# Attention scores from a two-half query: four terms stacked on 128 rows, or three terms on 64 rows with two heads side by side

## The chip, the core and the metric

The kernel runs on one NeuronCore of a Trainium2 chip. Five engines work from queues of their own, in order: TensorE (PE in the profile; its weight loads are the row PEld) multiplies, ScalarE (ACT) evaluates the exponentials and copies results out of the accumulators, VectorE (DVE) does elementwise work and reductions, GpSimd (POOL) issues the transfers that gather and scatter rows by index, and SyncE (SP) issues the plain transfers. Matmul results land in an accumulator memory, PSUM, of eight banks; everything else is in SBUF, whose 128 partitions are the rows of a tile. The metric is the device time of one launch in microseconds (us); lower is better.

## The reference

Sixteen batches of 1024 tokens with 512 features, 8 heads of width 64, and a 0/1 mask per token. The query is also the key and the value.

```python
xt = jnp.transpose(x, (0, 2, 1))
q = xt @ Wq.T
qh = q.reshape(B, T, NH, dk).transpose(0, 2, 1, 3)
scores = scale * jnp.einsum('bhqd,bhkd->bhqk', qh, qh)
logits = (scores * cmask + (1.0 - cmask) * NEG) * rmask
attn = jax.nn.softmax(logits, axis=-1)
ctx = jnp.einsum('bhqk,bhkd->bhqd', attn, qh)
out = ctx @ Wo.T
return x + jnp.transpose(out, (0, 2, 1))
```

A masked key takes no part, and a masked query averages over all keys, so the kernel computes attention for the unmasked tokens alone and gives every masked token the projected mean.

## The kernel before

Per batch the unmasked tokens (384 to 544 of 1024) are gathered into a tile of A = 544, 528 or 512 columns. PE transposes the rows (L486), multiplies by the query weights in float16 halves (L513: high times high, low times high, high times low), and ACT writes the float32 query `q`, 128 rows by A columns for each pair of heads e = 0..3 (head 2e in rows 0 to 63, head 2e+1 in rows 64 to 127).

`qsplit` (L521) cuts `q` into float16 halves: DVE casts the high half (L529), subtracts for the low half (L530) and copies the high half once more (L531), with a short extra copy (L534) where A is 528. Four DMAs on SP's queue (L540 to L543) then build `xx`, which holds for each head two stacks of 128 rows: high over low, and low over high. With these stacks as operands one matmul of 128 rows adds two of the four products of halves, so the scores of one head need two matmuls (a = 0, 1) for each half of the columns (g = 0, 1): four matmuls of A/2 columns (L701). Their result, `pss`, is one tile of two PSUM banks; the pool `ps_s` has two such tiles, used in turn. ACT takes the exponential out of it (L705), with the running sum read afterwards as an instruction of its own (ACTIVATION_READ_ACCUMULATOR), and the next scores that use that tile wait for it.

Each batch has 16 steps: a pair of heads p = 0..3 and a row block i = 0..3. In a step the scores of head 2p come first, then a part of the filling work (`fill`: queries, values and transposes of the next batch, projections of the previous one), then the scores of head 2p+1, then another part. The 16 matmuls of probabilities times values (`attend`, L726; two passes each in float32, so 32 records) run together at the second step of the next pair. They write 64 columns of the array each, two heads side by side, into the upper and lower halves of `pav`. Slots over 512 are the tail: their scores for four heads go together (L676, weights 32 columns wide, 16 matmuls, twice a batch in 14 batches). `value` (L559) makes the value tiles by multiplying both halves of `xx` by `two`, two identities of 64 columns on top of each other (L569, moving 64 columns, 8 per call). Program order within an engine is set by the tile framework when the kernel is built, from the order of the calls, priorities and its own estimates; on the chip every engine takes its queue in that order.

Of the kernel before, what the change touches and what calls it, by code (L numbers as in the profile page):

```python
# [19 lines left out]
P = 128  # L20
# [3 lines left out]
DK = 64  # L24
# [3 lines left out]
SCALE = 0.125  # L28
NEG = -1.0e30

C = 544
CT = C - 512
CQ = C + 2
HG = H // 2
# [12 lines left out]
class Fast:  # L47
# [91 lines left out]
    def setup2(self):  # L139
        nc, fixed = self.nc, self.fixed  # L140

        self.quad = fixed("quad", [P, HG])
        nc.vector.tensor_reduce(self.quad, self.ident.rearrange("p (r t) -> p r t", r=HG), AX.X, ALU.add)
        self.xh = fixed("xh", [P, DC, CQ], F16)
        self.xl = fixed("xl", [P, DC, CQ], F16)
        for t in (self.xh, self.xl):
            nc.gpsimd.memset(t[:, :, C + 1:], 0.0)

        self.rcol = [fixed("rcol%d" % k, [P, P]) for k in range(2)]
        self.smcol = [fixed("smcol%d" % k, [P, P]) for k in range(2)]  # L150
        for t in self.rcol + self.smcol:
            nc.gpsimd.memset(t, 0.0)

        self.two = fixed("two", [P, DK], F16)
        nc.vector.tensor_tensor(self.two, self.ident[:, :DK], self.ident[:, DK:], ALU.add)

        self.big = fixed("big", [P, self.B + 2 * DC])

        self.par = fixed("par", [P, 2])
        nc.vector.tensor_tensor(self.par, self.quad[:, 0:2], self.quad[:, 2:4], ALU.add)  # L160

        self.low = fixed("low", [P, 1])
        nc.vector.tensor_reduce(self.low, self.ident.rearrange("p (r k t) -> p k r t", r=HG, k=2)[:, 1], AX.XY, ALU.add)
        self.sign = fixed("sign", [P, 1])
        nc.vector.tensor_scalar(self.sign, self.low, -2.0, 1.0, ALU.mult, ALU.add)
# [243 lines left out]
            s["xt"] = self.rows(s["idx"][:s["A"] - 512, 4:5], self.sb([P, D], F32, "xt"))  # L409

    def start(self, b):
        s = self.st[b] = {"xa": [], "xx": [], "v": [], "c": [], "nm": [], "corr": [], "xm": []}
        s["ms2"] = self.sb([P, 2 * DC], F32, "ms2", 2)

    def load_half(self, b, k, after=None):
# [105 lines left out]
    def qsplit(self, b, e):  # L521


        nc, s = self.nc, self.st[b]
        A = s["A"]
        q = s["q"][:, e, :A]
        full = self.sb([P, 3, C], F16, "hl", 2)
        hl = full[:, :, :A]
        nc.vector.tensor_copy(hl[:, 0, :], q)  # L529
        nc.vector.tensor_tensor(hl[:, 1, :], q, hl[:, 0, :], ALU.subtract)  # L530
        nc.vector.tensor_copy(hl[:, 2, :], hl[:, 0, :])  # L531
        S = C if A > 512 else A
        if A < S:
            nc.vector.tensor_copy(full[:, :, A:], full[:, :, 512:A])  # L534
            hl = full
        xx = self.sb([P, 4, C], F16, "xx", 5)[:, :, :S]

        def spread():
            lo, up = slice(0, DK), slice(DK, P)
# [5 lines left out]
        self.later(spread)  # L545
        s["xx"].append(xx)

    def squares(self, v, dst, act=False, first=False):
        nc = self.nc
# [9 lines left out]
    def value(self, b, e):  # L559
        nc, s = self.nc, self.st[b]  # L560
        if e == 0:
            s["sd"] = self.sb([P, DC, H], F32, "sd")
        pv = self.pm([P, 4, P])
        for k in range(4):
            if b == 0:
                nc.tensor.transpose(pv[:, k, :], s["q"][:, e, k * P:(k + 1) * P], self.ident)
            else:
                for h in range(2):
                    nc.tensor.matmul(pv[:, k, h * DK:(h + 1) * DK], lhsT=s["xx"][e][:, 2 * h, k * P:(k + 1) * P],  # L569
                                     rhs=self.two, start=True, stop=True)  # L570
# [90 lines left out]
    def scores(self, b, p, i):  # L661


        nc, s = self.nc, self.st[b]
        A = s["A"]
        CH = A // 2
        if "z" not in s:
            s["z"] = self.sb([P, H, 4], F32, "z", 2)
            s["zt"] = self.sb([P, 2], F32, "zt", 2)
        if i is None:  # L670
            pt = self.ps_s.tile([P, 2, 512], F32, tag="s", name="pss")
            for a in range(2):
                for g in range(2):
                    for r in range(HG):
                        xx, k = s["xx"][2 * p + r // 2], r % 2
                        self.beat = nc.tensor.matmul(pt[r * CT:(r + 1) * CT, g, :CH], lhsT=xx[:, 2 * k, 512:C],  # L676
                                                     rhs=xx[:, 2 * k + a, g * CH:(g + 1) * CH],
                                                     start=(a == 0), stop=(a == 1)).ins
            t = self.sb([P, C], F32, "p", 12)[:, :A]
            nc.scalar.activation(t.rearrange("p (g c) -> p g c", g=2), pt[:, :, :CH], AF.Exp,  # L680
                                 bias=s["nm"][p][:, HG:], scale=SCALE, accum_out=s["zt"][:, p:p + 1])

            hi = self.sb([P, C], F32R, "c", 4)[:, :A]
            lo = t.bitcast(F32R)
            nc.vector.tensor_copy(hi, t)
            nc.vector.tensor_tensor(lo, t, hi.bitcast(F32), ALU.subtract)

            def spread():
                s["pt"] = self.sb([P, 2, C], F32R, "pt")[:, :, :A]
                half = slice(0, DK), slice(DK, P)  # L690
# [8 lines left out]
        for a in range(2):  # L699
            for g in range(2):  # L700
                self.beat = nc.tensor.matmul(pt[:, g, :CH], lhsT=xx[:, 2 * k, i * P:(i + 1) * P],  # L701
                                             rhs=xx[:, 2 * k + a, g * CH:(g + 1) * CH],
                                             start=(a == 0), stop=(a == 1)).ins
        t = self.sb([P, C], F32, "p", 12)[:, :A]
        self.exp = [nc.scalar.activation(t.rearrange("p (g c) -> p g c", g=2), pt[:, :, :CH], AF.Exp,  # L705
                                         bias=s["nm"][p // HG][:, p % HG:p % HG + 1], scale=SCALE,
                                         accum_out=s["z"][:, p, i:i + 1]).ins]
        return t

    def attend(self, b, p, i, ps):  # L710
        nc, s = self.nc, self.st[b]
# [221 lines left out]
    def run(self, flag):  # L933
        B = self.B
        L = lambda f, *a: lambda: f(*a)
        S = [(p, i) for p in range(NP) for i in range(4)]
# [21 lines left out]
        for i, e in enumerate(ends):  # L958
            g = list(range(ends[i - 1] + 1 if i else 0, e + 1))
# [36 lines left out]
        g1 = [(0, L(self.gather, 1, j)) for j in range(5)]  # L996

        def rest1():
            with self.behind(self.last_xx):
                for k in range(DC, 2 * DC):  # L1000
                    self.load_half(1, k)

# [32 lines left out]
        if True:  # L1035
            for b in range(B + 1):
                o, n = b - 1, b + 1
# [17 lines left out]
                if n < B:  # L1055
# [22 lines left out]
                    if b == 0:  # L1078
                        k = next(k for k, (c, f) in enumerate(m) if f is index[0][1])
# [40 lines left out]
                for st, (p, i) in enumerate(S):  # L1120
# [3 lines left out]
                    if i is None:  # L1124
                        if self.wide[b] > 512:
                            self.scores(b, p, None)
                    else:
                        ps = [self.scores(b, 2 * p, i)]
                        if i == 2 and whole:
                            whole.pop()()  # L1130
                    fill(share[st][0], st == N - 1)
                    if i is not None:
                        ps.append(self.scores(b, 2 * p + 1, i))

                    for _ in range(1 if b < B - 2 else -(-len(self.urgent + self.spare) // (N - st))):
                        self.issue()

# [165 lines left out]
```

## Time and profile before

| | |
|---|---|
| median of 2 runs | 1030.3 us (1029.69 and 1030.91) |
| span of the profiled execution | 1032.2 us |
| PE busy | 988.2 us (96%), 8455 matmuls |
| VectorE busy | 725.1 us (70%) |
| ScalarE busy | 659.5 us (64%) |
| GpSimd busy | 300.8 us (29%) |
| bytes moved by DMA | 177.73 MB |

The profile is one execution recorded on the chip. A group's row gives the line, the engine, the operation and its tiles, the count, the busy time, the mean duration of one, and the engine's idle time before it with what ended that idle time. A matmul's recorded duration includes the way through the array, which overlaps with the next matmul: what a matmul costs in a dense stretch is the distance from its start to the next start, and the timeline, which merges a run of equal instructions into one row (start, length from the first start to the last end, count), is the view to take it from. Idle time of an engine that is not the bottleneck costs nothing.

### The profile page before, as it was taken

Reading aid. Unit: us, or ns where it says so; the run is one execution under the profiler, and the core shown is the slowest. Engines: PE = TensorE matmul, PEld = TensorE weight load, DVE = VectorE, ACT = ScalarE, POOL = GpSimd, SP = SyncE. Lnnn points to the kernel's source line nnn. Section 1 sums busy time; section 2 is a strip of 40 time slices with the busy share of each in tenths; the row PEclk is TensorE's granted clock in tenths of the full one; section 3 lists DMA queues with packets and bytes.
Section 4 is the critical chain, followed back from the end, with each engine's and each line's share of the span. In section 5 each row is a group of like instructions: output and inputs, shape, how many; then the busy total and the mean of one; then the engine's idle time right before and its main releaser. Section 6 shows DMA issues by size and latency. Waiting matters only on the chain. (4 is left out here: it accounts for less than half of the span.)

```text
span 1032.2 us, 23511 instructions
## 1 busy us (share of the span) xinstructions
PE 988.2 (96%) x8455; PEld 685.0 (66%) x8455; DVE 725.1 (70%) x2410; ACT 659.5 (64%) x1702; POOL 300.8 (29%) x307
## 2 busy tenths in 40 slices
PE   7798999999999999999999999999999999999996
PEld 6576667666676766767666676767666666776563
DVE  6897668676775767877666787767777777666653
ACT  5876767557667666667667567756667667665550
POOL 3101013223311232233232333323232322325562
PEclk9999999999999999999999999999999999999999
DMA  6746546557554586575657565576565666556652
GB/s 199 231 139 183 136 134 161 183 161 206 165 142 128 150 239 172 151 209 148 190 157 227 172 169 168 163 203 185 163 210 138 192 184 184 151 142 191 185 183 95
DMA packets 78795, 177.73 MB, mean 172 GB/s; under 512 B 14688, under 2 KB 20576, under 8 KB 78672
## 3 DMA queue, kind: packets, MB, share of 16 engines
q1 hardware_dynamic: 57584, 108.40, 38.8%
q0 software_dynamic: 21088, 67.75, 20.9%
q8 instruction: 69, 1.13, 0.5%
q14 instruction: 54, 0.44, 0.1%
HBM read 91.49 MB, written 33.91 MB: 121 GB/s over the span
## 5 line engine op out<-in xcount | busy, mean ns | idle before, releaser
L705 ACT ACTIVATE p<-pss,nm 128x528 f32<-128x528 f32 (+2 forms) x512 | 359.5, 706 | 169.6 <-PE pss L701 160.0
L701 PE MATMUL pss<-xx 128*128 128x264 f16 (+2 forms) x2048 | 300.9, 276 | 6.1 <-ACT p L705 5.2
L726 PE MATMUL pav<-p,v 128*64 128x264 f32 (+2 forms) x2048 | 243.3, 390 | 0.0
L701 PEld LDWEIGHTS <-xx 128*128 128x128 f16 x2048 | 194.2, 99 | 62.4 <-issue 25.1
L726 PEld LDWEIGHTS pav<-p,v 128*64 128x64 f32 x2048 | 141.4, 137 | 85.7 <-issue 13.5
L901 POOL DMA_INDIRECT y_out<-xa,idx x68 | 73.5, 1081 | 285.4 <-PE pss L701 101.6
L513 PE MATMUL pm<-xh,wqh 128*128 128x264 f16 (+5 forms) x512 | 142.2, 278 | 4.1 <-DVE xa L822 3.4
L513 PE MATMUL pm<-xl,wqh 128*128 128x264 f16 (+5 forms) x512 | 141.6, 277 | 0.2 <-DVE xl L445 0.2
L513 PE MATMUL pm<-xh,wql 128*128 128x264 f16 (+5 forms) x512 | 141.7, 277 | 0.0
L395 POOL DMA_INDIRECT xa<-x_in,idx x68 | 68.6, 1009 | 201.7 <-PE pss L701 81.1
L513 PEld LDWEIGHTS <-wqh 128*128 128x128 f16 x1024 | 98.3, 99 | 24.0 <-issue 7.5
L705 ACT ACTIVATION_READ_ACCUMULATOR p<-pss,nm 128x1 f32 x512 | 103.9, 203 | 0.0
L901 POOL DMA_INDIRECT y_out<-xi,idx x60 | 72.6, 1211 | 97.0 <-PE pss L701 26.5
L817 PE MATMUL pm<-woh,ch 128*128 128x512 f16 x240 | 91.1, 379 | 0.0
L817 PE MATMUL pm<-woh,cl 128*128 128x512 f16 x240 | 90.9, 379 | 0.0
L817 PE MATMUL pm<-wol,ch 128*128 128x512 f16 x240 | 90.9, 379 | 0.0
L395 POOL DMA_INDIRECT xi<-x_in,idx x60 | 61.3, 1021 | 95.3 <-PE pss L701 31.9
L516 ACT ACTIVATE q<-pm 128x264 f32<-128x264 f32 (+5 forms) x128 | 50.2, 392 | 59.9 <-PE pm L513 59.3
L822 DVE SCALAR_TENSOR_TENSOR xa<-pm,xa 128x512 f32<-128x512 f32 x60 | 41.3, 689 | 56.4 <-PE pm L817 52.7
L817 PEld LDWEIGHTS <-ch 128*128 128x128 f16 x480 | 46.1, 98 | 44.8 <-issue 0.9
L799 DVE TENSOR_TENSOR c<-c,rb 128x528 f32<-128x528 f32 (+2 forms) x64 | 45.4, 710 | 43.0 <-DMA rb<-rd 21.3
L888 DVE TENSOR_TENSOR xi<-xi,ub 128x512 f32<-128x512 f32 (+1 forms) x60 | 40.8, 688 | 41.8 <-PE pss L701 41.2
(223 smaller groups left out, 1509.6 us busy)
## 6 DMA issues: line engine op xcount, KB each, us to landing
xx<-hl SPq DMA_DIRECT2D x224, 136.0 KB
xm<-x_nat_in SPq DMA_DIRECT2D x56, 512.0 KB
rb<-rd SPq DMA_DIRECT2D x72, 132.0 KB
rb<-rd SPq DMA_DIRECT2D x40, 136.0 KB
pt<-c SPq DMA_DIRECT2D x36, 132.0 KB
pt<-p SPq DMA_DIRECT2D x36, 132.0 KB
ub<-ud SPq DMA_DIRECT2D x16, 256.0 KB
xx<-hl SPq DMA_DIRECT2D x32, 128.0 KB
```

The source lines that it names most:

```text
L395: dma = self.nc.gpsimd.indirect_dma_start(out=tile[:n], out_offset=None, in_=self.x, in_offset=bass.IndirectOffsetOnAxis(ap=idx, axis=0))
L513: self.beat = nc.tensor.matmul(pq, lhsT=w[:, c, e * P:(e + 1) * P], rhs=xx[:, c, cols], start=(k == 0), stop=(k == 3 * DC - 1)).ins
L516: nc.scalar.activation(s["q"][:, e, cols], pq, AF.Copy, scale=1.0 / (SX * SW))
L701: self.beat = nc.tensor.matmul(pt[:, g, :CH], lhsT=xx[:, 2 * k, i * P:(i + 1) * P], rhs=xx[:, 2 * k + a, g * CH:(g + 1) * CH], start=(a == ...
L705: self.exp = [nc.scalar.activation(t.rearrange("p (g c) -> p g c", g=2), pt[:, :, :CH], AF.Exp, bias=s["nm"][p // HG][:, p % HG:p % HG + 1 ...
L726: mm = nc.tensor.matmul(s["pav"][k * DK:(k + 1) * DK, g, :CH], lhsT=s["v"][p][:, i, k * DK:(k + 1) * DK], rhs=ps[k][:, cols], start=(i == ...
L799: self.once(nc.vector.tensor_tensor(c[:, :A], c[:, :A], s["rb"][p], ALU.mult), self.beat if p < 3 else None)
L817: nc.tensor.matmul(po[:cols.stop - cols.start], lhsT=a[:, e, cols], rhs=w[:, e, :], start=(e == 0 and k == 0), stop=(e == DC - 1 and k == 2))
L822: self.nc.vector.scalar_tensor_tensor(x, po, 1.0 / (SX * SW), x, ALU.mult, ALU.add)
L888: self.once(self.nc.vector.tensor_tensor(x[:n], x[:n], s["ub"][:n], ALU.add), self.beat)
L901: dma = self.nc.gpsimd.indirect_dma_start(out=self.out, out_offset=bass.IndirectOffsetOnAxis(ap=idx, axis=0), in_=x, in_offset=None)
```

## The change

- `qsplit` writes the two halves, high and low, into `hl` (now 6 buffers, 2 slots) and nothing else: the second copy of the high half, the extra copy, the four DMAs and `xx` are gone.
- `scores` makes both heads of a pair in one call: three products of halves (high high, high low, low high; low low is left out, in this kernel's computation, as in its query and output products), each with 64 rows. For each product and each half of the columns the matmul of head 0 (rows 0 to 63) is followed by that of head 1 (rows 64 to 127). They write two `pss` tiles, and the two exponentials follow: 12 matmuls for two heads instead of 8.
- The loop calls `scores` once per step, ahead of the first part of the filling, instead of once before and once after it.
- For the tail, `qsplit` makes `tk` on VectorE: the tail columns of the halves times a 0/1 mask for the rows of one head, one instruction where A is 544 and two where it is 528. The tail scores then take 24 matmuls of 128 rows instead of 16.
- `value` adds two products with a 128-wide identity (moving 128 columns instead of 64), again 8 per call.

```diff
         q = s["q"][:, e, :A]
-        full = self.sb([P, 3, C], F16, "hl", 2)
-        hl = full[:, :, :A]
-        nc.vector.tensor_copy(hl[:, 0, :], q)
-        nc.vector.tensor_tensor(hl[:, 1, :], q, hl[:, 0, :], ALU.subtract)
-        nc.vector.tensor_copy(hl[:, 2, :], hl[:, 0, :])
...
-        xx = self.sb([P, 4, C], F16, "xx", 5)[:, :, :S]
...
-            nc.sync.dma_start(out=xx[lo, 0:2, :], in_=hl[lo, 0:2, :])
-            nc.sync.dma_start(out=xx[up, 0:2, :], in_=hl[lo, 1:3, :])
-            nc.sync.dma_start(out=xx[lo, 2:4, :], in_=hl[up, 0:2, :])
-            self.last_xx = nc.sync.dma_start(out=xx[up, 2:4, :], in_=hl[up, 1:3, :]).ins
...
+        hl = self.sb([P, 2, C], F16, "hl", 6)
+        nc.vector.tensor_copy(hl[:, 0, :A], q)
+        nc.vector.tensor_tensor(hl[:, 1, :A], q, hl[:, 0, :A], ALU.subtract)
+        s["hl"].append(hl)
+        if A > 512:
+            if e % 2 == 0:
+                s["tk"].append(self.sb([P, 2, 2, 2, CT], F16, "tk", 3))
+            n, st = A - 512, s["tk"][e // 2][:, e % 2]
+            for r in range(CT // n):
+                self.last_hl = nc.vector.tensor_tensor(
+                    st[:, :, :, r * n:(r + 1) * n], hl[:, :, 512:A].unsqueeze(2).broadcast_to([P, 2, 2, n]),
+                    self.par16.unsqueeze(1).unsqueeze(3).broadcast_to([P, 2, 2, n]), ALU.mult).ins
...
                 for h in range(2):
-                    nc.tensor.matmul(pv[:, k, h * DK:(h + 1) * DK], lhsT=s["xx"][e][:, 2 * h, k * P:(k + 1) * P],
-                                     rhs=self.two, start=True, stop=True)
+                    nc.tensor.matmul(pv[:, k, :], lhsT=s["hl"][e][:, h, k * P:(k + 1) * P], rhs=self.id16,
+                                     start=(h == 0), stop=(h == 1))
...
-        xx, k = s["xx"][p // 2], p % 2
-        pt = self.ps_s.tile([P, 2, 512], F32, tag="s", name="pss")
-        for a in range(2):
+        hl = s["hl"][p]
+        pts = [self.ps_s.tile([P, 2, 512], F32, tag="s", name="pss") for _ in range(2)]
+        for k, (a, c) in enumerate(((0, 0), (0, 1), (1, 0))):
             for g in range(2):
-                self.beat = nc.tensor.matmul(pt[:, g, :CH], lhsT=xx[:, 2 * k, i * P:(i + 1) * P],
-                                             rhs=xx[:, 2 * k + a, g * CH:(g + 1) * CH],
-                                             start=(a == 0), stop=(a == 1)).ins
...
+                for h in range(2):
+                    rows = slice(h * DK, (h + 1) * DK)
+                    self.beat = nc.tensor.matmul(pts[h][:, g, :CH], lhsT=hl[rows, a, i * P:(i + 1) * P],
+                                                 rhs=hl[rows, c, g * CH:(g + 1) * CH],
+                                                 start=(k == 0), stop=(k == 2)).ins
+        ts = []
+        for h in range(2):
+            t = self.sb([P, C], F32, "p", 12)[:, :A]
+            self.exp = [nc.scalar.activation(t.rearrange("p (g c) -> p g c", g=2), pts[h][:, :, :CH], AF.Exp,
...
-                        ps = [self.scores(b, 2 * p, i)]
+                        ps = self.scores(b, p, i)
                         if i == 2 and whole:
                             whole.pop()()
                     fill(share[st][0], st == N - 1)
-                    if i is not None:
-                        ps.append(self.scores(b, 2 * p + 1, i))
-
```

The tail's branch of `scores` loops over the same three products, with `tk` as the weights and `hl` as the moving operand.

More of the change, by code (lines that the diff above doesn't have):

```diff
@@ L152, in setup2 @@
             nc.gpsimd.memset(t, 0.0)
-        self.two = fixed("two", [P, DK], F16)
-        nc.vector.tensor_tensor(self.two, self.ident[:, :DK], self.ident[:, DK:], ALU.add)
+        self.id16 = fixed("id16", [P, P], F16)
+        nc.vector.tensor_copy(self.id16, self.ident)
         self.big = fixed("big", [P, self.B + 2 * DC])
@@ L160, in setup2 @@
         nc.vector.tensor_tensor(self.par, self.quad[:, 0:2], self.quad[:, 2:4], ALU.add)
+        self.par16 = fixed("par16", [P, 2], F16)
+        nc.vector.tensor_tensor(self.par16[:, 0:1], self.quad[:, 0:1], self.quad[:, 1:2], ALU.add)
+        nc.vector.tensor_tensor(self.par16[:, 1:2], self.quad[:, 2:3], self.quad[:, 3:4], ALU.add)
         self.low = fixed("low", [P, 1])
@@ L411, in start @@
     def start(self, b):
-        s = self.st[b] = {"xa": [], "xx": [], "v": [], "c": [], "nm": [], "corr": [], "xm": []}
+        s = self.st[b] = {"xa": [], "hl": [], "tk": [], "v": [], "c": [], "nm": [], "corr": [], "xm": []}
         s["ms2"] = self.sb([P, 2 * DC], F32, "ms2", 2)
@@ L671, in scores @@
             pt = self.ps_s.tile([P, 2, 512], F32, tag="s", name="pss")
-            for a in range(2):
+            for k, (a, c) in enumerate(((0, 0), (0, 1), (1, 0))):
                 for g in range(2):
                     for r in range(HG):
-                        xx, k = s["xx"][2 * p + r // 2], r % 2
-                        self.beat = nc.tensor.matmul(pt[r * CT:(r + 1) * CT, g, :CH], lhsT=xx[:, 2 * k, 512:C],
-                                                     rhs=xx[:, 2 * k + a, g * CH:(g + 1) * CH],
-                                                     start=(a == 0), stop=(a == 1)).ins
+                        self.beat = nc.tensor.matmul(pt[r * CT:(r + 1) * CT, g, :CH], lhsT=s["tk"][p][:, r // 2, a, r % 2, :],
+                                                     rhs=s["hl"][2 * p + r // 2][:, c, g * CH:(g + 1) * CH],
+                                                     start=(k == 0), stop=(k == 2)).ins
             t = self.sb([P, C], F32, "p", 12)[:, :A]
@@ L696, in scores @@
             return None
-        xx, k = s["xx"][p // 2], p % 2
-        pt = self.ps_s.tile([P, 2, 512], F32, tag="s", name="pss")
-        for a in range(2):
+        hl = s["hl"][p]
+        pts = [self.ps_s.tile([P, 2, 512], F32, tag="s", name="pss") for _ in range(2)]
+        for k, (a, c) in enumerate(((0, 0), (0, 1), (1, 0))):
             for g in range(2):
[L701 to L708, printed above, removed]
+                for h in range(2):
+                    rows = slice(h * DK, (h + 1) * DK)
+                    self.beat = nc.tensor.matmul(pts[h][:, g, :CH], lhsT=hl[rows, a, i * P:(i + 1) * P],
+                                                 rhs=hl[rows, c, g * CH:(g + 1) * CH],
+                                                 start=(k == 0), stop=(k == 2)).ins
+        ts = []
+        for h in range(2):
+            t = self.sb([P, C], F32, "p", 12)[:, :A]
+            self.exp = [nc.scalar.activation(t.rearrange("p (g c) -> p g c", g=2), pts[h][:, :, :CH], AF.Exp,
+                                             bias=s["nm"][p // 2][:, p % 2 * 2 + h:p % 2 * 2 + h + 1], scale=SCALE,
+                                             accum_out=s["z"][:, 2 * p + h, i:i + 1]).ins]
+            ts.append(t)
+        return ts
     def attend(self, b, p, i, ps):
@@ L998, in rest1 @@
         def rest1():
-            with self.behind(self.last_xx):
+            with self.behind(self.last_hl):
                 for k in range(DC, 2 * DC):
```

8 lines of the change are left out of this document (removed).

## The prediction

> **What bounds the kernel now.** I read the page's busy times and slices first, then the groups, then the waits, then the timeline of PE and of ACT in dense stretches.
>
> ```profile
> span 1032.2 us, 23511 instructions
> ...
> PE 988.2 (96%) x8455; PEld 685.0 (66%) x8455; DVE 725.1 (70%) x2410; ACT 659.5 (64%) x1702; POOL 300.8 (29%) x307
> ...
> PE   7798999999999999999999999999999999999996
> ```
>
> PE is busy in every slice between the start and the end, and no other engine is over 70%. So the time is PE's queue: the distances between its starts, plus the places where it waits. The page's chain of waits says nothing here: it ends in the last 1.57 us. What could bound it next is ACT, through one dependency: a score tile is free again only when its exponential and the read of its sum are done.
>
> ```profile
> L705 ACT ACTIVATE p<-pss,nm 128x528 f32<-128x528 f32 (+2 forms) x512 | 359.5, 706 | 169.6 <-PE pss L701 160.0
> L701 PE MATMUL pss<-xx 128*128 128x264 f16 (+2 forms) x2048 | 300.9, 276 | 6.1 <-ACT p L705 5.2
> L705 ACT ACTIVATION_READ_ACCUMULATOR p<-pss,nm 128x1 f32 x512 | 103.9, 203 | 0.0
> ```
>
> Today ACT waits 160.0 us for scores, and PE stands idle only 5.2 us for exponentials. The timeline gives the prices. Its columns are start, length from first start to last end, then engine, line and operation with the count.
>
> ```profile
> 481.09 0.61 PE L701 MATMUL pss<-xx 128*128 128x264 f16 x4
> 481.63 0.41 PE L486 MATMUL pm<-ident,xt 16*128 16x16 f32 x4
> 481.98 0.29 PE L513 MATMUL pm<-xh,wqh 128*128 128x264 f16 x1
> ...
> 503.30 1.06 PE L701 MATMUL pss<-xx 128*128 128x264 f16 x8
> 504.29 3.78 PE L726 MATMUL pav<-p,v 128*64 128x264 f32 x32
> 508.00 1.07 PE L701 MATMUL pss<-xx 128*128 128x264 f16 x8
> 508.91 0.28 PE L513 MATMUL pm<-xh,wqh 128*128 128x264 f16 x1
> ...
> 516.48 0.38 PE L817 MATMUL pm<-wol,ch 128*128 128x512 f16 x1
> 516.70 0.38 PE L817 MATMUL pm<-woh,cl 128*128 128x512 f16 x1
> 517.01 0.63 PE L676 MATMUL pss<-xx 128*32 128x264 f16 x16
> 517.57 0.33 PE L628 MATMUL pm<-ident,smcol 128*128 128x128 f32 x1
> ```
>
> A score matmul of 264 columns lasts 276 ns, but eight of them take 1.06 us: (1.06 - 0.276)/7 = 0.112 us from start to start. Two more things are to be seen. Narrow tiles run side by side: the 16 tail matmuls at 517.01, with weights 32 columns wide, take 0.63 us; less 0.28 for the length of the last one that is 0.35 from the first start to the last, three sets of four on, so a set of four (0.117) costs what one full matmul costs. And a change of tile shape has a price. From 503.30 to 504.29 are 0.99 us for eight matmuls worth 8 x 0.112 = 0.896: 0.094 us on entering the 64-column shape, where 508.00 to 508.91 (0.91, no change of shape) shows almost none. From 516.70 to 517.01 are 0.31 instead of the 0.22 between 516.48 and 516.70 (0.09 again), from 517.01 to 517.57 are 0.56 for four sets worth 0.45 (0.11 on leaving), and into the 16-row transposes at 481.63 it is 0.54 - 4 x 0.112 = 0.09. So a shape with fewer rows pays it as one with fewer columns does.
>
> **The change part by part.** I write each term as it moves the 1032.2 us of the profiled execution.
>
> *Score matmuls, -57 us.* Before: 2048 x 0.112 = 229 us. After, 3072 matmuls in pairs on rows 0 to 63 and 64 to 127: if a pair costs one matmul, 1536 x 0.112 = 172. No row shows two row halves at work together, so the bounds are 172 (side by side, as the column tiles at 517.01) and 344 (one after the other). I take 172, since that row is the same array cut the other way and is shared by four.
>
> *Values, +12.5 us; tail, +6.3 us.*
>
> ```profile
> 9.09 3.12 PE L363 MATMUL warm<-on 128*128 128x128 f16 x53
> ...
> 252.78 0.40 PE L569 MATMUL pm<-two,xx 128*128 128x64 f16 x8
> ```
>
> ```profile
> L569 PE MATMUL pm<-two,xx 128*128 128x64 f16 x480 | 24.9, 193 | 1.6 <-DMA xx<-hl 1.3
> L363 PE MATMUL warm<-on 128*128 128x128 f16 x120 | 10.4, 259 | 0.0
> L486 PE MATMUL pm<-ident,xt 16*128 16x16 f32 (+1 forms) x52 | 5.5, 218 | 0.4
> ```
>
> A value matmul of 64 columns costs (0.40 - 0.193)/7 = 0.029 us, with the mean of one from its group's row; one of 128 columns costs (3.12 - 0.259)/52 = 0.055. There are 480: 480 x 0.026 = 12.5. The tail gets two more sets of four, 28 times: 56 x 0.112 = 6.3.
>
> *Changes of shape, +55 us.* In the order of the built kernels I counted the places where PE goes from one tile shape to another: 196 before, 778 after. Every score call now enters the half-row shape and leaves it, and 63 of the 256 are cut in two or more by filling work, which adds further changes. 582 x 0.094 = 55. Bounds: 0, if cutting the rows in two is free, and 582 x 0.11 = 64. I take 0.094: the 16-row transposes pay it.
>
> *Waits for the exponentials, +38 us and +9 us.* This is the wait that the change adds. Both heads now end together and both score tiles are in use at once, so PE's next score call waits for two exponentials in a row, where before it waited for one, with a whole head's scores between.
>
> ```profile
> 503.95 0.70 ACT L705 ACTIVATE p<-pss,nm 128x528 f32<-128x528 f32 x1 [1.00 <-PE pss L701]
> 504.55 0.19 ACT L705 ACTIVATION_READ_ACCUMULATOR p<-pss,nm 128x1 f32 x1
> 504.64 0.69 ACT L705 ACTIVATE p<-pss,nm 128x528 f32<-128x528 f32 x1
> 505.23 0.20 ACT L705 ACTIVATION_READ_ACCUMULATOR p<-pss,nm 128x1 f32 x1
> 505.32 1.05 ACT L425 ACTIVATE xm<-xm 128x1024 f32<-128x1024 f32 x1
> ```
>
> Two exponentials with their reads take 505.43 - 503.95 = 1.48 us. The last score matmul starts 0.276 before its end; with some 0.07 us for the two hand-overs (the fourth matmul of 503.30 ends at 503.91 and ACT starts at 503.95), the second tile is free 0.276 + 1.48 + 0.07 = 1.83 us after that start. Of this PE fills 0.112 with the matmul itself and 2 x 0.094 with the two changes of shape, so a wait arises wherever less than 1.53 us of other work lies between two score calls. I summed that work over the built order with the distances above (0.112 for 264 columns, 0.216 for 512, 0.055 for values, 0.11 for a float32 transpose, 0.226 for a pair of `attend` passes): of 255 gaps 117 hold less than 1.53 us, many just one half query (12 x 0.112 = 1.34), and what they lack adds up to 51 us. The same count on the order before, with one exponential (0.276 + 0.79 + 0.07 - 0.112 = 1.03 us, from one call to the next but one), gives 15 us. I take 53 - 15 = 38, with 2 us for the wider batches. Queued behind the waiting matmul is all of PE's work, so each such wait moves the end. Bounds: 0, if ACT's and PE's queues drift so that the short gaps lie behind long ones, and 70, if other ACT work falls between: the row at 505.32 shows a sum of 1.05 us, plus 0.2 for its read, right behind a pair. A score call that starts as the second tile comes free ends some 0.9 us later, so such a sum holds the next exponential up by 0.35; there are 56, and with 117 of 255 gaps short that is 9 us.
>
> *The start, -5 us; tail transfers, -3 us.*
>
> ```profile
> 38.23 0.29 PE L676 MATMUL pss<-xx 128*32 128x272 f16 x2 [1.00 <-ACT p L705]
> 41.73 0.28 PE L676 MATMUL pss<-xx 128*32 128x272 f16 x1 [3.22 <-DMA xx<-hl]
> ...
> 44.40 0.43 PE L513 MATMUL pm<-xh,wqh 128*128 128x274 f16 x1
> ```
>
> The wait of 3.22 us for the stacks goes, and with it about nine matmuls at double the length after it (0.43 instead of 0.28): 9 x 0.11 = 1; the rest is for the smaller waits of the first batches. What is late next there is ACT's exponential, the 1.00 us of the row above.
>
> ```profile
> L730 PE MATMUL pav<-pt,vt 128*128 128x272 f32 (+1 forms) x152 | 33.1, 318 | 6.1 <-DMA pt<-p 6.0
> L531 DVE COPY hl<-hl 128x528 f16<-128x528 f16 (+2 forms) x64 | 18.7, 291 | 0.0
> L534 DVE COPY hl<-hl 128x48 f16<-128x48 f16 x36 | 6.2, 172 | 0.4
> ```
>
> ```profile
> xx<-hl SPq DMA_DIRECT2D x224, 136.0 KB
> ```
>
> These transfers leave SP's queue, 224 x 136 KB and 32 smaller ones. Away from the start PE waits for DMA only at the tail's `pt`, 6.0 us; I give half of it. VectorE loses 18.7 + 6.2 us of copies and gains 92 small products; at the 172 ns of the shortest copy that is 16 us. It is 70% busy and PE hardly waits for it, so this costs nothing either way; without that cover it would be 9 us gained.
>
> Sum: 1032.2 - 57 + 12.5 + 6.3 + 55 + 38 + 9 - 5 - 3 = 1088. The two timed runs have a median of 1030.3, 1.9 below the profiled span, so I forecast 1086, 5% slower: what the pairs save, the changes of shape take back, and the two exponentials in a row come on top.
>
> **The rivals.** *Half-row tiles without a price for the change (not slower).* If cutting the rows in two does not drain the array, 55 us go: 1031. For it: no row here shows exactly two halves of 64. Against it: 481.63 and both column shapes pay 0.09. It decides from under about 0.03 us a change (1086 - 582 x 0.06 = 1051).
>
> *The exponentials stay hidden.* Without the 47 us of waits it is 1039. For it: PE waited only 5.2 us in the old order. Against it: a static order with 117 short gaps. Together with the first rival it would be 984, the one way that I see to a clear gain.
>
> *Weights not hidden in half rows.* The loads of the next pair may not get behind the running pair. Nearest rows: 0.029 us a load and matmul at 252.78 (64 columns), and 0.064 for a 16-row transpose at 481.63, (0.41 - 0.218)/3. Over 1536 pairs that is 45 to 98 us: 1131 to 1184. Against it: the tail's 32-column sets load four weights each and lose nothing. [...]
>
> *No side by side.* Pairs one after the other: 1086 + 1536 x 0.112 = 1258. [...]
>
> **How the numbers follow.** Forecast 0.51; free changes 0.15; hidden exponentials 0.11; both 0.06; unhidden weights 0.11; no side by side 0.06. The range takes in the bounds of the two big terms and most of the neighbours: 1030 to 1150, leaving out "both", "no side by side" and the far end of the unhidden weights, some 0.2. Two per cent, about what a measurement here can tell from no change, is 1010 to 1051. Faster: "both" and the luckier parts of the two single rivals, 0.12. Within: most of those two, 0.17. Slower: 0.71.
>
> **What would show it.** Score matmuls in the timeline as rows of 12 with about 0.95 us (6 x 0.112 + 0.276): right; 1.6 us: no side by side; 1.1 to 1.3: weights. The distance from the last score matmul to the next of another line, and into the first: 0.09 more than its columns. The row "PE pss <- ACT p" among the waits: from 5.2 to some 40 us. PE's first wait for `xx` gone. If PE's busy time falls by 57 and its idle time stays, the two added prices were wrong.

## The result and the profile after

The changed kernel takes 1114.5 us (median of 2 runs, 1113.58 and 1115.4) where the kernel before takes 1030.3: a ratio of 1.0818 [1.0787, 1.0849], 8% slower. The forecast was 1086, 5% slower, with a range to 1150. A later measurement, with the kernel before run again beside it, gave 1.0806 [1.0766, 1.0847].

The first rows of the page of the kernel after: span, busy times, and the two groups that the change is about (idle time of the engine and what ended it at the end of a row).

```profile
span 1113.7 us, 25464 instructions
...
PE 1058.5 (95%) x9703; PEld 669.9 (60%) x9703; DVE 738.2 (66%) x2404; ACT 661.2 (59%) x1702; POOL 301.5 (27%) x307
...
L703 ACT ACTIVATE p<-pss,nm 128x528 f32<-128x528 f32 (+2 forms) x512 | 356.1, 701 | 170.5 <-PE pss L697 167.3
L697 PE MATMUL pss<-hl 64*128 64x264 f16 (+2 forms) x3072 | 279.3, 277 | 16.9 <-ACT p L703 14.5
```

PE is still the engine that sets the time. It is busy for 70.3 us more (1058.5 against 988.2) and idle for 11.2 us more (1113.7 - 1058.5 = 55.2, against 44.0). The prediction had it the other way round: some 17 us more of work and changes of shape, and 39 more of waits. The wait for exponentials went from 5.2 to 14.5 us, not to 40.

The timeline of PE in a dense stretch (start, length from first start to last end, line, operation, count) shows the new score calls in the form that was meant:

```profile
544.75 0.38 PE L816 MATMUL pm<-woh,cl 128*128 128x512 f16 x1
545.06 0.85 PE L697 MATMUL pss<-hl 64*128 64x264 f16 x12
545.84 3.78 PE L725 MATMUL pav<-p,v 128*64 128x264 f32 x32
549.55 0.85 PE L697 MATMUL pss<-hl 64*128 64x264 f16 x12
550.34 0.29 PE L516 MATMUL pm<-xh,wqh 128*128 128x264 f16 x1
```

Twelve matmuls in 0.85 us: less the 0.277 of one that is 0.57 for five further pairs, 0.115 a pair, the price of one matmul before. So the two heads do run side by side, and nothing of their weight loads shows. Entering costs 0.09 (545.06 - 544.75 = 0.31, where such a projection is otherwise followed after 0.22), and leaving 0.11 (0.78 from 545.06 to 545.84, less six pairs of 0.112). Other calls in the same timeline look like this:

```profile
560.86 0.84 PE L697 MATMUL pss<-hl 64*128 64x264 f16 x6
561.64 0.29 PE L516 MATMUL pm<-xh,wqh 128*128 128x264 f16 x1
561.86 0.85 PE L697 MATMUL pss<-hl 64*128 64x264 f16 x6
...
572.08 1.51 PE L697 MATMUL pss<-hl 64*128 64x264 f16 x12 [0.16 <-ACT p L703]
```

Here six matmuls take as long as twelve did, and twelve take 1.51: (1.51 - 0.277)/11 = 0.112 for each. These are six of one head and then six of the other, and at 560.86 a query matmul stands between them. The program order, which the framework sets when the kernel is built, has taken the pairs apart.

To see how much there is of this I went through all of PE's starts in both traces. A pair is two matmuls of the two heads that start less than 30 ns apart. Of 1536 possible pairs 1068 exist; about 125 more start 30 to 100 ns apart and overlap in part, and the rest of the matmuls run alone. Counted by the pairs that start together, with each of the other 3072 - 2 x 1068 = 936 matmuls on its own, the scores take up to 1068 + 936 = 2004 turns of 0.112 us, and not 1536; before there were 2048. The same pass splits each span: every distance to the next start is the work of the first instruction at the rates of the prediction, plus 0.094 where the shape changes, plus what a halved clock adds where the records show one; the rest is waits.

| us | before | after | difference | in the prediction |
|---|---|---|---|---|
| work | 920.2 | 929.5 | +9.3 | -57 + 12.5 + 6.3 = -38 |
| changes of shape | 20.9 (222) | 74.3 (790) | +53.4 | +55 |
| lost at half clock | 3.2 | 14.5 | +11.3 | not there |
| waits | 76.3 | 82.5 | +6.2 | 38 + 9 - 5 - 3 = +39 |
| before the first and after the last start | 11.6 | 13.0 | +1.4 | not there |
| span | 1032.2 | 1113.7 | +81.6 | +56 |

The third row has its counterpart in the mean clock that the profile gives for each run, first before, then after:

```profile
core 0: 1032.2 us, clock 0.995
```

```profile
core 0: 1113.7 us, clock 0.984
```

The timeline shows where it sets in. A stop of PE for an exponential, and another for a maximum, are followed by query matmuls at twice their distance (0.22 us from 527.75 to 527.97, against 0.11 from 527.03 to 527.14):

```profile
525.99 0.27 PE L697 MATMUL pss<-hl 64*128 64x264 f16 x1 [0.91 <-ACT p L703]
526.79 0.39 PE L632 MATMUL pm<-ident,m 128*128 128x4 f32 x2 [0.53 <-DVE m L625]
527.03 0.27 PE L516 MATMUL pm<-xh,wqh 128*128 128x264 f16 x1
527.14 0.27 PE L516 MATMUL pm<-xl,wqh 128*128 128x264 f16 x1
...
527.75 0.43 PE L516 MATMUL pm<-xh,wqh 128*128 128x264 f16 x1
527.97 0.43 PE L516 MATMUL pm<-xl,wqh 128*128 128x264 f16 x1
```

### The profile page after: what moved, and what is told of

The parts are those of the page before. It is cut to its first block, busy times and chain, and to the rows that moved or that the text cites. A ratio compares the mean times of both kernels' runs of the same rounds, so it can differ in the third digit from the quotient of the medians.

```text
span 1113.7 us, 25464 instructions
## 1 busy us (share of the span) xinstructions
PE 1058.5 (95%) x9703; PEld 669.9 (60%) x9703; DVE 738.2 (66%) x2404; ACT 661.2 (59%) x1702; POOL 301.5 (27%) x307
## 5 line engine op out<-in xcount | busy, mean ns | idle before, releaser
L697 PE MATMUL pss<-hl 64*128 64x264 f16 (+2 forms) x3072 | 279.3, 277 | 16.9 <-ACT p L703 14.5
L697 PEld LDWEIGHTS <-hl 64*128 64x128 f16 x3072 | 160.8, 95 | 98.5 <-issue 62.2
L516 PE MATMUL pm<-xh,wqh 128*128 128x264 f16 (+5 forms) x512 | 146.0, 285 | 4.9 <-DVE idx L331 2.7
L516 PE MATMUL pm<-xl,wqh 128*128 128x264 f16 (+5 forms) x512 | 144.7, 283 | 0.2 <-DVE xl L448 0.2
L516 PE MATMUL pm<-xh,wql 128*128 128x264 f16 (+5 forms) x512 | 144.6, 282 | 0.0
L516 PEld LDWEIGHTS <-wqh 128*128 128x128 f16 x1024 | 94.5, 100 | 45.0 <-issue 28.0
L398 POOL DMA_INDIRECT xa<-x_in,idx x68 | 75.8, 1114 | 165.2 <-ACT qt L576 41.2
L900 POOL DMA_INDIRECT y_out<-xi,idx x60 | 66.4, 1106 | 107.2 <-PE pm L516 39.2
L816 PEld LDWEIGHTS <-ch 128*128 128x128 f16 x480 | 42.8, 98 | 51.5 <-issue 9.1
```

What stands on the lines that cost most here:

```text
L398: dma = self.nc.gpsimd.indirect_dma_start(out=tile[:n], out_offset=None, in_=self.x, in_offset=bass.IndirectOffsetOnAxis(ap=idx, axis=0))
L516: self.beat = nc.tensor.matmul(pq, lhsT=w[:, c, e * P:(e + 1) * P], rhs=xx[:, c, cols], start=(k == 0), stop=(k == 3 * DC - 1)).ins
L697: self.beat = nc.tensor.matmul(pts[h][:, g, :CH], lhsT=hl[rows, a, i * P:(i + 1) * P], rhs=hl[rows, c, g * CH:(g + 1) * CH], start=(k == 0 ...
L816: nc.tensor.matmul(po[:cols.stop - cols.start], lhsT=a[:, e, cols], rhs=w[:, e, :], start=(e == 0 and k == 0), stop=(e == DC - 1 and k == 2))
L900: dma = self.nc.gpsimd.indirect_dma_start(out=self.out, out_offset=bass.IndirectOffsetOnAxis(ap=idx, axis=0), in_=x, in_offset=None)
```

## The experiments

Ratios are to the kernel before, run beside each group: its median was 1040.9 us for the first four, 1042.6 for the next four and 1031.4 for the last four, so ratios and not times are compared across groups.

**1. The pairs tied together.** Every score matmul of a call is put directly behind the one before it in the program order.

```diff
+        last = None
         for k, (a, c) in enumerate(((0, 0), (0, 1), (1, 0))):
...
-                    self.beat = nc.tensor.matmul(pts[h][:, g, :CH], ...
+                    with ExitStack() as st:
+                        if last is not None:
+                            st.enter_context(self.behind(last))
+                            st.enter_context(self.tc.high_priority(offset=HPO))
+                        last = self.beat = nc.tensor.matmul(pts[h][:, g, :CH], ...
```

> The changed kernel with the 12 score matmuls of a call tied together in their order, so that head 1 follows head 0 at once. In the changed kernel's trace only 1068 of the 1536 possible pairs start together, so the scores take 2004 slots of 0.112 us instead of 1536. Theory A (lost pairs): the lone matmuls are a cost of their own; nearly all pairs come back, some 450 slots x 0.112 = 50 us go, and the time falls from 1114 to between 1062 and 1085, depending on how much PE then waits. Theory B (the two exponentials in a row are the cost, and the lone matmuls only fill that wait): the row 'PE pss <- ACT p' grows from 14.5 us by about as much as the slots save, and the time stays at 1105 to 1115.

Measured: 1.0717 [1.0673, 1.0762], some 10 us less than the changed kernel's 1.0818. The pairs came: 1381 of 1536 start together, 1691 turns instead of 2004, which by this count is 35 us of PE's time. Most of it went elsewhere. The waits for exponentials, from the view of waits (total, times, longest), and the clock:

```profile
PE pss L702 <- ACT p L708: 26.2, 29, 4.1
```

```profile
core 0: 1117.6 us, clock 0.973
```

By the split above, against the changed kernel (measured when the kernel before was 1% faster): work -32, waits before scores +15 (26.0 to 41.4), other waits +11, half clock +11. The built order of this kernel has 80 gaps shorter than 1.53 us that lack 32.7 us in all, by the prediction's count; 41.4 measured is of that size, which by itself does not show that the count has the cause (experiments 6 and 10). The changed kernel's order does not keep its pairs: where six matmuls of head 0 run before six of head 1, the first exponential can start 0.67 us earlier, and the second tile comes free that much sooner after the last matmul. That lost pairs and waits are largely the same time in two forms is an argument from the sizes; what this run shows is that undoing the one brings the other.

**2. Two exponentials in a row, with nothing else.** The kernel before, with both heads' scores called together; stacks, values and tail as they were.

```diff
-                        ps = [self.scores(b, 2 * p, i)]
+                        ps = [self.scores(b, 2 * p, i), self.scores(b, 2 * p + 1, i)]
...
-                    if i is not None:
-                        ps.append(self.scores(b, 2 * p + 1, i))
```

> The kernel before with both heads' scores called together ahead of the filling; stacks, DMAs and the eight 128-row matmuls as before, no change of shape. The prediction's step for the waits (two exponentials in a row, 38 + 9 us) gives 1077. If the built order gets round most of these waits, as the changed kernel's trace suggests (waits up by some 6 us in all), it is 1030 to 1045.

Measured: 1.0092 [1.0063, 1.012], 9.5 us and not 47.

```profile
PE pss L701 <- ACT p L705: 12.3, 15, 2.4
```

The row rises from 5.2 to 12.3 us: the mechanism is there, at a fifth of the size. The test is milder than the step it tests, though: here head 0's four matmuls still end 4 x 0.112 = 0.45 us before head 1's, so the first exponential can start that much sooner than where both heads end together.

**3. The price of a change of shape, alone.** The kernel before, with every second score matmul on rows 0 to 63 only, so that its shape changes inside each call. No matmul is added.

```diff
-                                             rhs=xx[:, 2 * k + a, g * CH:(g + 1) * CH],
+                rows = slice(0, DK if a else P)
...
+                                             rhs=xx[rows, 2 * k + a, g * CH:(g + 1) * CH],
```

> The kernel before with the second of each pair of stacked score matmuls (a = 1) run on rows 0 to 63 alone, which leaves out the product of low and high halves; same count and columns, nothing side by side, but 512 score calls that each enter and leave the half-row shape. Theory: a change of shape costs 0.094 us wherever it falls, so 1024 x 0.094 = 96 us: 1126, or down to 1105 if PE's other waits shrink. Rival (a change is hidden by work in flight or absorbed by waits that were there anyway): under 1050.

Measured: 1.0781 [1.074, 1.0823], 80 us for 1198 - 222 = 976 more changes: 0.082 us each. The timeline has two calls in one row of eight (two of 128 rows, two of 64, and again):

```profile
506.22 1.38 PE L702 MATMUL pss<-xx 128*128 128x264 f16 x8
507.53 0.39 PE L818 MATMUL pm<-woh,ch 128*128 128x512 f16 x1
```

Eight such matmuls took 1.06 us before; 1.38 holds three changes more, (1.38 - 1.06)/3 = 0.11. This settles the first rival: rows cut in two pay like columns cut in two. The 80 us are net of some waits that shrank:

```profile
PE pss L702 <- ACT p L706: 3.0, 4, 1.8
PE pav L731 <- DMA pt<-p: 2.1, 1, 2.1
```

These were 5.2 and 6.0 us before; with those 6 us added back a change costs (80 + 6)/976 = 0.088. The rows of the weight loads show where the price lies:

```profile
506.19 0.13 PEld L702 LDWEIGHTS <-xx 128*128 128x128 f16 x2
506.54 0.11 PEld L702 LDWEIGHTS <-xx 64*128 64x128 f16 x2 [0.22 <-issue]
506.86 0.11 PEld L702 LDWEIGHTS <-xx 128*128 128x128 f16 x2 [0.22 <-issue]
```

Within a shape a load starts 1 to 2 ns (median) after the start of the matmul ahead of it, and so runs under it; the first load after a change starts 201 to 204 ns after that start (medians behind matmuls of 264 or 266 columns, in the kernel before, the changed one and this one), and its matmul some 4 ns later. 0.204 less the 0.112 at which the next matmul would have come is the price of 0.09.

**4. The values alone.** The kernel before, with the values made by two 128-wide identity products.

```diff
-                    nc.tensor.matmul(pv[:, k, h * DK:(h + 1) * DK], lhsT=s["xx"][e][:, 2 * h, k * P:(k + 1) * P],
-                                     rhs=self.two, start=True, stop=True)
+                    nc.tensor.matmul(pv[:, k, :], lhsT=s["hl"][e][:, h, k * P:(k + 1) * P], rhs=self.id16,
+                                     start=(h == 0), stop=(h == 1))
```

> The kernel before with only the values changed: two products with a 128-wide identity from the tile of halves, 128 moving columns instead of 64. By 480 x 0.026 us it is 12.5 us slower, 1043. If PE's waits for other engines absorb it: 1030 to 1035. If the values gain by no longer waiting for the stacks' DMAs: below 1030.

Measured: 1.0065 [1.0046, 1.0083], 6.7 us. The group in this run's view by lines:

```profile
L570 PE MATMUL pm<-id,hl 128*128 128x128 f16 x480 | 36.9, 220 | 1.5 <-DVE xl L445 1.5
```

Against the 24.9 us of the group before, busy time rises by 12.0, as priced; the split has 12.1 more work and 3.6 less waiting (72.7 against 76.3). So 6.7 of the 12.5 reach the end, and the shorter waits make up for most of the rest.

**5. The pairs tied, and the filling shared out evenly** between the steps, to lengthen the short gaps.

```diff
-                share = [(1.2, 0) if i is None else ((1.0, 0.6), (0.1, 0.5), (0.9, 1.0), (0.9, 0.9))[i] for _, i in S]
+                share = [(1.2, 0) if i is None else ((1.1, 0.9), (0.0, 0.0), (1.0, 1.0), (1.0, 0.9))[i] for _, i in S]
```

> The tied pairs of e1_chain, and the filling work spread so that none of it stands at the second step of a pair, where the value products already lie between two score calls: parts 1.1 and 0.9, 0 and 0, 1 and 1, 1 and 0.9 instead of 1 and 0.6, 0.1 and 0.5, 0.9 and 1, 0.9 and 0.9. The count on the built order gives 37 us lacking in 74 gaps, against 33 us in 80 gaps for e1_chain, since a half query is 1.36 us and cannot be cut: so the count says no gain, ratio to the kernel before 1.06 to 1.08 (e1_chain 1.072). If the waits come from the filling parts being uneven: 1.04 to 1.05.

Measured: 1.0669 [1.0636, 1.0702], not told apart from experiment 1. The built order has 74 short gaps that lack 37 us, as much as before.

**6 and 7. Without the running sums of the exponentials**, in the kernel of experiment 1 and in the kernel before as its control.

```diff
+            nc.vector.memset(s["z"], 300.0)
+            nc.vector.memset(s["zt"], 300.0)
...
-                                             bias=s["nm"][p // 2][:, p % 2 * 2 + h:p % 2 * 2 + h + 1], scale=SCALE,
-                                             accum_out=s["z"][:, 2 * p + h, i:i + 1]).ins]
+                                             bias=s["nm"][p // 2][:, p % 2 * 2 + h:p % 2 * 2 + h + 1], scale=SCALE).ins]
```

> The tied pairs of e1_chain, without the sums that the exponentials accumulate (the sums are a constant instead, so the division that normalises is left out in effect): two exponentials in a row then take about 1.1 us instead of 1.48, and the wait arises under some 1.15 us of other work instead of 1.53. If the second exponential's lateness is what holds PE: the count falls from 33 us lacking to about 14, the half-clock stretches that follow PE's stops (61 us of them in e1_chain) mostly go, 10 to 15 us, and the ratio falls from 1.072 to 1.04 to 1.05. If the score waits come from elsewhere: above 1.065, no more than the control e7 gains.

> Control for e6: the kernel before without the accumulated sums (constants instead). One exponential then takes about 0.6 us instead of 0.79; by the count 15 us lacking become some 8, so a ratio of 0.99 to 1.0. If ACT were a bound of the kernel before, well under 0.98.

Measured: 1.0618 [1.0568, 1.0668], and 0.9946 [0.9925, 0.9967] for the control. Relative to experiment 1 that is 1%, of which the control accounts for half. The second tile came free 1.35 us after the scores' end (median) instead of 1.51: a read overlaps more than half of its 0.2 us with the exponentials beside it (in the prediction's rows it runs from 504.55 to 504.74 us, the one exponential to 504.65, the next from 504.64), so taking two away shortened the wait by only 0.16. Over 80 short gaps that is 13 us by the count; what came beyond the control is 0.0045, some 5 us, which the intervals do not tell from nothing.

**8. A later first tail**, in the kernel before: the first batch's tail scores after its fourth step, where PE waited 3.22 us for the stacks.

```diff
+                S.insert(2 if b else 4, (0, None))
+                S.insert(13, (1, None))
```

> The kernel before with the first batch's first tail scores called after its fourth step instead of after its second, so that PE does not stand 3.22 us at the start for the DMA of the second stack, nor run nine matmuls at half clock after it. If nothing else is late there: 3 to 5 us off, ratio 0.995 to 0.997. If ACT's exponentials are next, as they were in the changed kernel, which has no such DMA and began its first value products at 53.27 us instead of 51.15: no change, 0.999 to 1.002.

Measured: 0.998 [0.996, 1.0]: no gain that can be told from none. In the kernel after, too, that wait is gone without a gain. In this run the waits for exponentials rose from 5.2 to 13.1 us:

```profile
PE pss L701 <- ACT p L705: 13.1, 14, 3.7
```

In the changed kernel exponentials are late at that place, too (timeline of PE, after):

```profile
39.42 0.88 PE L670 MATMUL pss<-hl,tk 128*32 128x272 f16 x24 [1.02 <-ACT p L703]
40.23 0.86 PE L697 MATMUL pss<-hl 64*128 64x272 f16 x6
42.65 1.26 PE L697 MATMUL pss<-hl 64*128 64x272 f16 x6 [1.55 <-ACT p L674]
```

**9. The changed kernel again**, beside the last three.

> The changed kernel once more, on the same chip as the three runs beside it, so that ratios can be set side by side: 1.079 to 1.085 as on the first chip.

Measured: 1.0806 [1.0766, 1.0847].

**10 and 11. A later second exponential**: a copy of 96 columns on ScalarE between the two exponentials of a call (in the control, after the first head's), in the kernel of experiment 1 and in the kernel before.

```diff
+            if h == 0:
+                with self.behind(*self.exp):
+                    nc.scalar.copy(self.idle, self.on16[:, :96])
```

> The tied pairs of e1_chain with a copy of 96 columns on ACT (some 0.25 us, result unused) behind the first of the two exponentials of a call, so that the second score tile comes free some 0.2 us later. If the second exponential's lateness holds PE: 76 to 80 short gaps x 0.2 = 15 us and a few more half-clock stretches, ratio 1.072 to 1.085 to 1.10. If PE's waits come from elsewhere: as e1_chain, 1.067 to 1.076.

> Control for e10: the same copy in the kernel before, behind every other exponential (the same 256 copies). Its scores are called head by head with filling between, and 66 of its 510 gaps are short; half of them follow a copy: 33 x 0.2 = 7 us, ratio 1.005 to 1.01. If the load on ACT alone slows a kernel of this kind as much as e10: over 1.015.

Measured: 1.0764 [1.0717, 1.0812], and 1.0065 [1.0042, 1.0088] for the control. Experiment 1 had 1.0717 [1.0673, 1.0762]: the intervals overlap, and the difference is no more than the control's. The second tile did come free later, 1.68 us after the scores' end (median) instead of 1.51. Had that lateness held PE at all of some 80 short gaps, 80 x 0.17 = 14 us would have made it 1.085. The row of waits went the other way, from 26.2 in experiment 1 to:

```profile
PE pss L703 <- ACT p L709: 17.3, 27, 1.5
```

**12. Without ScalarE's sums over whole rows**, in the kernel of experiment 1: the 1.05 us instructions behind the prediction's term of 9 us.

```diff
-        with self.behind(*self.exp):
-            self.nc.scalar.activation(s["xm"][k], s["xm"][k], AF.Copy, accum_out=s["ms2"][:, k:k + 1])
+        if k == 0:
+            self.nc.vector.memset(s["ms2"], 0.0)
```

> The tied pairs of e1_chain without ACT's 62 sums over whole rows of 1.05 us (the mean of all tokens is left out, a constant stands in its place). The prediction gave such sums behind a pair of exponentials 9 us: ratio from 1.072 to 1.06. In e1_chain one pair in ten is done over 2.4 us after its scores instead of 1.5; if these sums are the reason, the half-clock stretches go as well: down to 1.05. If they fall where PE has slack: 1.067 to 1.076.

Measured: 1.1047 [1.0997, 1.1096], slower, with less for ScalarE to do. The view of waits for this run, whole span:

```profile
PE pss L702 <- ACT p L708: 16.4, 32, 1.4
PE pm L632 <- DVE m L625: 13.3, 10, 2.3
PE pm L516 <- DVE nm L634: 11.2, 4, 6.3
```

The wait that was aimed at did fall, from 26.2 to 16.4 us; but in experiment 10, with more for ScalarE to do, it had fallen as far, so the fall cannot be put down to the sums. Waits for VectorE's preparation of the batches grew: for `m` from 4.6 to 13.3 (15.0 in experiment 10), and for `nm` from nothing to 11.2, 10.5 us of it between 30 and 200 us of the span. The clock was lower as well:

```profile
core 0: 1132.6 us, clock 0.966
```

The starts of the value products tell where. In experiment 1 the 257th of them starts at 194.0 us and the 1921st at 1056.5, 862.5 us on; here at 218.1 and 1072.7, 854.6 on; in experiment 10 at 194.4 and 1046.2, 851.8 on. Divided by the median of the kernel before beside each, the three stretches are 0.829, 0.829 and 0.826. So all of this kernel's loss lies in the first batches, where its order puts PE behind VectorE, and in the steady part neither less work on ScalarE nor more of it moved the time. As far as these two changes go, what the steady stops cost is not set by how soon ScalarE is done with other things.

## Why the prediction was right, and which steps were not

The sign and the range held, on the mechanism that carries most of it, the changes of shape. That the size came as near as 5% for 8% is luck in part: the score matmuls saved some 47 us less than forecast, and the waits cost some 33 us less.

*Changes of shape, +55: right.* 568 more on the chip (790 against 222) where 582 were counted, 53.4 us in the split, and experiment 3 prices them by itself at 0.08 to 0.11. The rival that made them free is refuted, by itself and together with hidden exponentials. That a change drains the array, as that rival's condition has it, no trace shows; what they show is the late load of experiment 3, 201 to 204 ns after the start of the matmul ahead instead of 1 to 2.

*Score matmuls, -57: the step "if a pair costs one matmul, 1536 x 0.112 = 172" failed, in its count.* A pair does cost one matmul, so "no side by side" and "weights not hidden" are refuted (the first by the rows of twelve in 0.85 us, the second by their 0.115 a pair; for that row I had written 0.95, one turn too many). The loads of the next pair go to the same two row halves and run while the pair ahead is at work: in the row at 545.06, from the third pair on, each starts 1 to 2 ns after the matmul of its head in the pair ahead and lasts 94 ns, and the pairs follow each other at 0.11 us. But only 1068 of 1536 pairs start together. In the split the scores saved 12.5 + 6.3 - 9.3 = 9.5 us, so some 47 of the 57 never came (468 turns of 0.112 would be 52, but about 125 of the missing pairs overlap in part). Much of this could have been read beforehand: in the built order 1196 pairs stand together, the rest are taken apart. I counted the changes of shape in that order, and took the pairs from the diff.

*Waits, +38 and +9: mechanism there, size wrong.* Waits before scores went from 18.2 to 26.0 us. The pair of exponentials alone costs 9.5 us (experiment 2); with the pairs kept together it is 41.4 - 18.2 = 23 (experiment 1), where the count for that order gives 32.7 - 15 = 18. That they agree does not make the count right: the second tile 0.16 us earlier (experiment 6) or 0.17 later (experiment 10) moved the time by no more than can be told from the controls. For the changed kernel's own order the count gave 53, since it assumed that both heads end together in every call; 139 of the 256 calls run as six pairs, the others out of step or, wholly or in part, one head after the other. The separate 9 us for ScalarE's other work are not supported: experiments 10 and 12 changed that work both ways without an effect in the steady part.

*Half clock, +11: a term that was not in the sum.* It is larger where PE stops more: 3.2, 14.5 and 25.9 us in the kernel before, the changed one and experiment 1, whose clocks are 0.995, 0.984 and 0.973; experiment 12 has 0.966. No run changed it by itself, so that the stops cause it is not shown.

*Values +12.5, tail +6.3: the work as priced*, but experiment 4 shows that 6.7 of the 12.5 reach the end. *The start, -5: wrong sign.* The first value products begin at 53.27 instead of 51.15 us; the wait for the stacks gave way to waits for exponentials, as the step itself had feared. *Tail transfers, -3:* the wait for `pt` is gone whole (its 6.0 us to nothing). That the missing transfers did this is not shown: it is gone in experiment 2 as well, which keeps them all.

Still open: what the remaining stops before scores hang on. They are few and long (in the changed kernel 34 over 0.15 us make 20.3 of 26.0), and six of them, 1.03 or 1.04 us each, follow a single transpose of line 623 that stands alone between two score calls, in six of the batches; that is a short gap as the prediction meant it. Tying the matmuls, sharing the filling and changing ScalarE's load each moved such stops to other places. No version of the change that was run beats the kernel before.

## What to carry to other kernels

Side by side is a property of the built order, not of the source: count the pairs that stand next to each other there before crediting them, as one counts the changes of shape. A tile shape used for 0.7 us at a time paid about 0.09 us on the way in and again on the way out (0.09 and 0.11 in the row at 545.06, 0.08 to 0.11 a change in experiment 3), so group the small-shape work into long runs or leave it. And where PE is busy throughout, its stops may cost twice, once as the stop and once as the slower clock that was seen behind some of them (14.5 us lost at half clock in the changed kernel, 3.2 in the kernel before).

## What the runs showed of the hardware that was not expected

Two matmuls on the two row halves shared the array fully: 0.115 us for two of 264 columns, where one of 128 rows took 0.112, their starts 3 ns apart (median of the 1068 pairs), with weights loaded anew for each (9703 loads for 9703 matmuls on the page). Where the shape changed, the next weights were loaded late: their load started 0.201 to 0.204 us after the start of the matmul ahead instead of 1 to 2 ns (medians, experiment 3), which accounts for the 0.09 us.

The half clock was also recorded behind short stops: in the rows at 525.99 PE had stood still for 0.91 + 0.53 us, and the half clock (0.50 granted, 1.00 until then) began at 527.64, some 0.8 us after the second stop, and lasted 3.4 us. Not every such stop is followed by it. Of the six equal ones behind line 623 two were, so something besides their length decides; what it is stays open. The stretches recorded in the middle of the changed kernel's span are 3.4 us long (from 527.6, 599.3, 664.2 and 732.4 us) or 10.2 (from 182.9); why they have these lengths is not shown.
